# A three-line reordering in the first attention of a vision-transformer tower: where side work stands among a chunk's score matmuls

## The chip, the core and the metric

The kernel runs on one core of a Trainium2 chip. The core has five engines that run their own instruction streams in order and meet only at semaphores: TensorE (PE in the profile: matmuls and transposes, with its weight loads shown as PEld), VectorE (DVE), ScalarE (ACT), GpSimd (POOL) and SyncE (SP, which here only issues DMAs). The metric is the time on the device in microseconds, median over several executions.

## The reference, cut to what matters

The whole program is a tokenizer (two convolutions), an attention with ReLU scores, an attention per expert, a linear attention and a mixture-of-experts feed-forward, on 128 images with 64 tokens of 256 features. The change touches only the first attention:

```python
h = h + _L0_attn_ref(_layernorm(h, axis=-1), Wq, Wk, Wv, w_mlp, b_mlp)

def _L0_attn_ref(x, Wq, Wk, Wv, w_mlp, b_mlp):      # B=128, L=64, 8 groups of 32 features
    Q, K, V = x @ Wq.T, x @ Wk.T, x @ Wv.T
    Qg = Q.reshape(B, L, 1, G, Dg)
    Kg = K.reshape(B, 1, L, G, Dg)
    diff = Qg - Kg
    attn = jnp.einsum('bqkgd,d->bqkg', jax.nn.relu(diff), w_mlp) + b_mlp[0]
    attn = jax.nn.relu(attn)
    attn = jax.nn.softmax(attn, axis=2)
    Vg = V.reshape(B, L, Dg, G)
    out = jnp.einsum('bqkg,bkdg->bqdg', attn, Vg)
    return out.reshape(B, L, d_att)
```

A score is thus not a product of query and key. For every pair of tokens it is a weighted sum over 32 features of ReLU(query - key). These differences are elementwise work for VectorE, GpSimd and ScalarE, and TensorE sums them over the features.

## The kernel before, in words

`relu_attention` (lines 307 to 767) works on eight blocks of 16 images. A block has eight chunks of eight query tokens each, so there are 64 chunks, and one loop (line 708, variable `n`) runs over them. Loop `n` computes the scores of chunk `n`, and beside them the softmax of chunk `n - 1` (`old`) and the queries of chunk `n + 1`. The whole loop is written in an order fixed by hand (`tc.manual_schedule()`): every engine carries out its share of the steps in the order of the program text.

**The scores of a chunk.** 16 images times two halves of the features give 32 parts. A part is `m`, a tile of query-key differences, and it comes in one of three ways: `larger` (line 527; VectorE, max of query and key, L530, for images 0 to 7 and images 12 and 13 of the second half), `difference` (line 534; GpSimd subtracts, L538, and ScalarE applies the ReLU in place, L539) and `by_query` (line 543; ScalarE alone, four instructions of L548 per call). `begin` (line 523) starts the sum `sc` in PSUM with a full-array matmul (L525), and eight calls of `add` (line 556) sum four parts each with matmuls in 32-column strips of the array (L340, eight instructions in the trace per call). `add(i, hf)` reads the parts of images `i` to `i + 3` of feature half `hf`. `add(12, 1, True)` ends a chunk's scores.

**The softmax of the chunk before.** `less_max` (L564 to L566, VectorE) reads the finished `sc`; `exponents` (L571, ScalarE); `sums` (L574, L575, VectorE); `weights` (L578, GpSimd); `transpose` (L587, TensorE: 32 instructions in 64-column strips into a PSUM tile `pt`); `transposed` (L595, ScalarE copies it out).

**The queries of the chunk after.** `queries` (L463, TensorE, eight full-array instructions into `pc`) and `queried` (L474, ScalarE copies a part of them for GpSimd and `by_query`).

**The work of blocks.** What is done once per block is cut into steps and hung into the loops: `at(n, place, ...)` notes it, and `do(n, place)` carries it out. The places are letters. X, Y and Z hold TensorE steps. O, A, B and C hold ScalarE steps, mostly the copies out of PSUM of what X, Y and Z made, and normalisations. V1 and V2 hold VectorE steps. W holds GpSimd factors. From loop 4 to loop 59 the contents repeat every eight loops; written for loops 28 to 35:

| loop | X | Y | Z | A | others |
|---|---|---|---|---|---|
| 28 | keys (0,0) | | keys (1,0) | copies X | O copies a transpose; C normalises |
| 29 | keys (0,1) | | keys (1,1) | copies X | O copies Z of 28; C normalises |
| 30 | values 0 | key_sums | | copies X | O copies Z of 29; C normalises |
| 31 | values 1 | | values 2 | copies X | V1 correction; C normalises |
| 32 | transpose 0 | values 3 | transpose 1 | copies X | O copies Z of 31; B copies Y; V1 offsets |
| 33 | outcome 0 | outcome 1 | | copies half of X | O copies Z of 32; B and C copy more |
| 34 | back 0 | back 1 | transpose 2 | normalises | O copies the last outcome; B normalises; V2 adds |
| 35 | back 2 | back 3 | transpose 3 | normalises | O copies Z of 34; B normalises; V1 and V2 add |

Keys are four matmul instructions of 512 columns (L409), values eight of 256 (L428), a transpose four of 128 (L397), `back` four of 128 (L502), all on the full array; `outcome` is 128 small ones on 64x32 pieces (L484); key_sums are 36 in 32-column strips. From loop 43 on, the expert attention hangs its first steps into the same places (lines 1187 to 1217): the loads of its weights (loop 55, Z, L807 to L815: one memset on GpSimd and six DMAs issued by SyncE; loop 57, Z, L822: two DMAs), `wt.values` (58, Z, L833), its router's logits (61, X, L955), the first pair's queries and keys (61 Z and 62 X, L1019) and values (62 Z and 63 X, L1041). The values of loop 63 are read in that loop's V1 by VectorE (`values_kept(1)`, L1055).

**Buffers.** X, Y, Z and the transposes of the weights take their PSUM tiles from one ring of four (`sh.ps`, line 303, tag "pq"). The parts of `difference` and of the last `larger` share five buffers (`mgp`), the other `larger` have three (`mvp`), `by_query` three (`map_`), `sc` two.

**The order on each engine in one loop**, before the change:

- TensorE: `add(0,0)`, X, `add(8,0)`, `add(4,0)`, queries, Y, `add(8,1)`, `add(0,1)`, `add(4,1)`, `begin` of the next chunk, transposes of the weights, `add(12,0)`, Z, `add(12,1)`.
- ScalarE: ReLU(8,0), O, by_query(14) first half, ReLU(10,0), exponents, by_query(14) second half, ReLU(8,1), A, ReLU(10,1), queried, B, by_query(15) first half, ReLU(12,0), by_query(15) second half, ReLU(14,0), the copy of the transposed weights, C.
- VectorE: larger(0,0), larger(4,0), less_max, V1, larger(0,1), sums, larger(4,1), larger(12,1), V2.
- GpSimd: difference(8,0), (10,0), (8,1), (10,1), (12,0), weights, W, difference(14,0).

Of the kernel before, what the change touches and what calls it, by code (L numbers as in the profile page):

```python
# [306 lines left out]
def relu_attention(c, sh, wqkv, wmlp, bmlp, beside):  # L307
# [10 lines left out]
    with (  # L318
# [288 lines left out]
        def first(x):  # L607

            for half in range(2):
                for n in range(4 * half, 4 * half + 4):  # L610
                    x.statistics(n)
                x.factors(4 * half, 4 * half + 4)
            for half in range(2):
                x.offsets(4 * half, 4 * half + 4)
            for n in range(4):
                x.normal(n)
                x.normal(4 + n, True)
            for i in (0, 2, 1, 3):
                x.transpose(i)
                x.transposed(i, i > 1)  # L620
            for s in range(2):
                x.keys(s, 0)
                x.keyed(s, 0, s == 1)
            x.queries(0)
            x.queried(0)

        def first_rest(x):
            for s in range(2):
                x.keys(s, 1)
                x.keyed(s, 1, True)  # L630
            x.key_sums()
            x.correction()

        for b, x in enumerate(blocks):
            n = 8 * b
# [64 lines left out]
        def do(n, place):  # L700
            for step in work.pop((n, place), ()):
                step()

        with tc.manual_schedule():
            seq = [(x, q0) for x in blocks for q0 in range(0, T, 8)]
            first(blocks[0])
            ch, old = Chunk(*seq[0]), None
            for n in range(len(seq)):
                new = None
                ch.difference(8, 0)  # L710
                ch.larger(mvp, 0, 4, 0)
                do(n, "O")
                if n == 0:
                    first_rest(blocks[0])
                    ch.begin()
                ch.by_query(14, 1, 0)
                ch.add(0, 0)
                do(n, "X")
                ch.difference(10, 0)
                ch.add(8, 0)  # L720
                ch.larger(mvp, 4, 4, 0)
                ch.add(4, 0)
                if old:
                    old.less_max()
                    old.exponents()
                ch.by_query(14, 1, 1)
                if n + 1 < len(seq):
                    seq[n + 1][0].queries(seq[n + 1][1])
                ch.difference(8, 1)
                do(n, "A")  # L730
                do(n, "V1")
                do(n, "Y")
                ch.difference(10, 1)
                if n + 1 < len(seq):
                    seq[n + 1][0].queried(seq[n + 1][1])
                    new = Chunk(*seq[n + 1])
                do(n, "B")
                ch.by_query(15, 1, 0)
                ch.add(8, 1)
                ch.larger(mvp, 0, 4, 1)  # L740
                ch.add(0, 1)
                if old:
                    old.sums()
                ch.difference(12, 0)
                if old:
                    old.weights()
                do(n, "W")
                ch.by_query(15, 1, 1)
                ch.larger(mvp, 4, 4, 1)
                ch.add(4, 1)  # L750
                if new:
                    new.begin()
                if old:
                    old.transpose()
                ch.larger(mgp, 12, 2, 1)
                do(n, "V2")
                ch.difference(14, 0)
                if old:
                    old.transposed()
                do(n, "C")  # L760
                ch.add(12, 0)
                do(n, "Z")
                ch.add(12, 1, True)
                old, ch = ch, new
            old.less_max()
# [1403 lines left out]
@with_exitstack  # L2169
def vit_tower(ctx: ExitStack, tc: tile.TileContext, a, out):  # L2170
    const = ctx.enter_context(tc.tile_pool(name="const", bufs=1))
    dram = ctx.enter_context(tc.tile_pool(name="dram", bufs=1, space=DRAM))
    c = Ctx(tc, const)

    hd = dram.tile([B, T, D], F32, name="hd")

    hx = dram.tile([B, T, D], F32, name="hx")
    gfd = dram.tile([B * T, 1], F32, name="gfd")
    with tc.tile_pool(name="stream", bufs=1) as sp:
        c.h2 = sp.tile([P, B // 2, D], F32, name="h2")  # L2180
        tokenizer(c, a["x"], a["w1"], a["bn1"], a["w2"], a["bn2"])
        with ExitStack() as rings:
            sh = Shared(c, rings)
            beside, rest = expert_attention(
                c, sh, hd, *(a[k] for k in ("normw", "wr", "br", "wqkvf", "wvf", "wproj", "bproj", "wout"))
            )
            rest(*relu_attention(c, sh, a["wqkv0"], a["wmlp"], a["bmlp"], beside))
    c.tables(ctx.enter_context(tc.tile_pool(name="tables", bufs=1)))
    with tc.tile_pool(name="gate", bufs=1) as gp:
        k = Routing(c, gp, a["wg"], a["bg"])  # L2190
        linear_attention(c, hd, hx, out, k, a["wqk1"], a["bqk1"], a["wv1"], a["bv1"], a["wg"])
        experts(c, hx, gfd, out, a["we1"], a["we2"], a["be2"], lambda: route(c, k, gfd))
# [71 lines left out]
```

## Time and profile before

| what | us |
|---|---|
| median of 7 executions (2690.27 to 2695.7) | 2692.04 |
| the profiled execution, its own time | 2694.02 |
| its span, first to last instruction | 2692.3 |
| mean granted TensorE clock in it | 0.982 |
| VectorE's wait for scores (L564 for L340), 202 to 1110 us | 46.7 |
| TensorE busy, 560.1 to 673.7 us (eight loops, 113.6 us) | 112.45 |
| VectorE busy in the same stretch | 106.55 |
| ScalarE busy in it | 99.82 |
| GpSimd busy in it | 99.84 |

The start of `less_max` (L564) marks the loops best, since it is where VectorE meets TensorE. From the timeline, with the idle time of VectorE just before it:

| loop | start of less_max | until the next | idle before it |
|---|---|---|---|
| 28 | 601.49 | 15.16 | none |
| 29 | 616.65 | 14.59 | 1.21 |
| 30 | 631.24 | 12.97 | 1.72 |
| 31 | 644.21 | 14.86 | none |
| 32 | 659.07 | 14.59 | 1.66 |
| 33 | 673.66 | 13.30 | none |
| 34 | 686.96 | 14.00 | 0.44 |
| 35 | 700.96 | 14.11 | 0.47 |
| 36 | 715.07 | | none |

In the lines of the timeline below, the first number is the start in us from the start of the span, the second the busy time of the row, then the engine, the line of the program, the operation, output and input, their shapes and how many instructions the row merges. In brackets stands the idle time before it and what released it. A matmul row's busy time overlaps the next row a little, since matmuls are pipelined; the distance from start to start (the "step") is what TensorE spends.

### The profile page before, as it was taken

What the parts mean: (1) busy time and instruction counts of PE and PEld (TensorE: products, weight loads), DVE (VectorE), ACT (ScalarE), POOL (GpSimd) and SP (SyncE); (2) the same over time, 40 slices, a digit from 0 to 9 for tenths busy, and PEclk for the clock granted to TensorE, in tenths of its full rate; (3) what the DMA queues carried; (4) which work ended last, traced back from release to release, by engine and by line L of the source; (5) the groups of instructions that cost most, each with busy time, mean ns of one, the idle gap of its engine ahead of it and who ended that gap; (6) DMA issues with size and microseconds to landing.
All of it is one profiled execution on the core that took longest, in us unless ns stands there. A gap on an engine that the chain in (4) does not pass through costs nothing.

```text
span 2692.3 us, 80911 instructions
## 1 busy us (share of the span) xinstructions
PE 2545.4 (95%) x35229; PEld 1721.7 (64%) x35229; DVE 2025.6 (75%) x3028; ACT 1627.6 (60%) x3421; POOL 1616.5 (60%) x1381
## 2 busy tenths in 40 slices
PE   8989999999999999999999999999799986999997
PEld 4553444444443444588888888888466565888886
DVE  5759999999999989888877878777367686444443
ACT  2228888888888988766666666666245533232332
POOL 3318888888888988666666566653132312445544
PEclk9999999999999999999999999999899998999998
DMA  3100000000000000000000000000435444555554
GB/s 111 32 13 1 2 2 2 1 2 1 2 2 1 2 12 2 3 12 19 11 12 19 12 19 11 11 19 11 118 64 125 94 119 149 178 196 188 196 187 135
DMA packets 138271, 141.14 MB, mean 52 GB/s; under 512 B 107875, under 2 KB 121701, under 8 KB 130224
## 3 DMA queue, kind: packets, MB, share of 16 engines
q1 hardware_dynamic: 127536, 118.40, 14.8%
q0 software_dynamic: 7648, 14.77, 1.8%
q8 instruction: 278, 4.55, 0.7%
q10 hardware_dynamic: 2720, 2.69, 0.3%
q14 instruction: 89, 0.73, 0.1%
HBM read 104.03 MB, written 32.54 MB: 51 GB/s over the span
## 4 chain that ended last, share of the span: by engine, by line
PE 70%; DVE 19%; issue 5%; ACT 4%; POOL 2%; DMA 1%; DVEq 0%; POOLq 0%; SPq 0%; ACTq 0%
PE sc L340 12%; PE po L2108 6%; DVE m L530 6%; PE ph L2092 6%; PE pc L184 5%; PE pt L1102 4%; PE pqk L1019 4%; PE sc L1066 4%; PE pq L1426 4%; PE pv L1041 3%; PE pz L1115 3%; PE pt L587 2%; PE sc L525 2%; DVE mx L1078 2%; PE pv L1440 2%
## 5 line engine op out<-in xcount | busy, mean ns | idle before, releaser
L538 POOL TENSOR_TENSOR m<-q,k 128x1024 f32<-128x1024 f32 x384 | 718.8, 1904 | 28.8 <-PE sc L340 14.3
L530 DVE TENSOR_TENSOR m<-pc,k 128x2048 f32<-128x2048 f32 (+1 forms) x320 | 647.0, 2057 | 0.5 <-ACT q L474 0.5
L340 PE MATMUL sc<-m,wide 128*32 128x512 f32 x4096 | 528.6, 599 | 14.1 <-DVE m L530 8.9
L539 ACT ACTIVATE m<-m 128x1024 f32<-128x1024 f32 x384 | 402.7, 1050 | 10.3 <-POOL m L538 9.7
L340 PEld LDWEIGHTS sc<-m,wide 128*32 128x32 f32 x4096 | 126.2, 109 | 254.8 <-issue 140.8
L548 ACT ACTIVATE m<-k,q 128x64 f32<-128x64 f32 x1024 | 270.8, 339 | 0.9 <-DVE k L421 0.9
L1078 DVE TENSOR_REDUCE mx<-sc 128x16 f32<-128x1024 f32 x128 | 156.0, 1219 | 134.2 <-PE sc L1066 134.2
L1093 POOL TENSOR_TENSOR e<-e,mx 128x1024 f32<-128x1024 f32 x128 | 243.5, 1902 | 10.0
L1025 ACT COPY kr<-pqk 128x512 f32<-128x512 f32 x254 | 137.9, 604 | 141.1 <-PE pqk L1019 141.1
L2092 PE MATMUL ph<-xt,w1s 128*128 128x256 f32 x896 | 198.8, 380 | 3.7 <-DVE xt L2083 2.7
L2108 PE MATMUL po<-w2s,hT 128*128 128x256 f32 x896 | 198.0, 379 | 0.0
L1092 POOL TENSOR_TENSOR mx<-mx,gate 128x16 f32<-128x16 f32 x128 | 27.6, 216 | 277.7 <-ACT z L1123 162.2
L2092 PEld LDWEIGHTS ph<-xt,w1s 128*128 128x128 f32 x896 | 169.8, 190 | 28.3 <-DVE xt L2083 3.3
L2108 PEld LDWEIGHTS po<-w2s,hT 128*128 128x128 f32 x896 | 168.1, 190 | 21.7
L1105 ACT COPY pT<-pt 128x512 f32<-128x512 f32 x256 | 139.0, 600 | 51.3 <-PE pt L1102 51.1
L1079 DVE TENSOR_TENSOR e<-sc,mx 128x1024 f32<-128x1024 f32 x128 | 156.7, 1224 | 4.4
L2126 POOL DMA_INDIRECT out<-y,rout x56 | 56.7, 1013 | 167.8 <-ACT hT L2096 124.8
L1085 DVE TENSOR_REDUCE mx<-e 128x16 f32<-128x1024 f32 x128 | 152.5, 1191 | 4.6 <-ACT e L1082 4.4
L1102 PE MATMUL pt<-ident,e 128*128 128x128 f32 x1024 | 143.0, 282 | 10.3 <-DVE vr L1055 7.3
L2096 ACT ACTIVATE hT<-ph,w1s 128x256 f32<-128x256 f32 x224 | 93.0, 470 | 96.9 <-PE ph L2092 96.9
L2113 ACT ACTIVATE y<-y,gf 128x256 f32<-128x256 f32 x56 | 28.0, 507 | 196.5 <-issue 107.6
L1082 ACT ACTIVATE e<-e 128x1024 f32<-128x1024 f32 x128 | 139.6, 1091 | 1.6 <-DVE e L1079 1.6
(330 smaller groups left out, 5011.2 us busy)
## 6 DMA issues: line engine op xcount, KB each, us to landing
w1s<-in_we SPq DMA_DIRECT2D x30, 1028.0 KB, 5.2
w2s<-in_we SPq DMA_DIRECT2D x30, 1024.0 KB, 4.9
hd<-h SPq DMA_DIRECT2D x16, 512.0 KB, 3.2
x<-hd SPq DMA_DIRECT2D x16, 512.0 KB, 3.9
h<-hd SPq DMA_DIRECT2D x4, 2048.0 KB, 12.7
hx<-h SPq DMA_DIRECT2D x4, 2048.0 KB, 11.8
out<-h SPq DMA_DIRECT2D x4, 2048.0 KB, 20.6
xt<-in_x SPq DMA_DIRECT2D x15, 512.0 KB, 3.6
```

The costliest lines, as they stand in the source:

```text
L340: nc.tensor.matmul(dst[j : j + 32], wide[:, hf, s : s + 32], part, start=start, stop=stop)
L530: nc.vector.tensor_tensor(m, bcast(self.pq[:, hf, i : i + n], 3, T), k, ALU.max)
L538: nc.gpsimd.tensor_tensor(m, bcast(self.q[:, hf, s : s + 2], 3, T), k, ALU.subtract)
L539: nc.scalar.activation(m, m, AF.Relu)
L548: nc.scalar.activation(self.parts[i, hf][:, q], self.blk.k[:, hf, i], AF.Relu, bias=self.q[:, hf, i - NB // 2, q : q + 1], scale=-1.0,)
L1078: nc.vector.tensor_reduce(mx, sc, AX.X, ALU.max)
L1079: nc.vector.tensor_sub(e, sc, bcast(mx, 2, T))
L1085: nc.vector.tensor_reduce(self.sm[x], self.e[x], AX.X, ALU.add)
L1093: nc.gpsimd.tensor_mul(e, e, bcast(sm, 2, T))
L1102: nc.tensor.transpose(pt[:, cq, :], e[:, i : i + 2, :].rearrange("p e s -> p (e s)"), c.ident)
L2092: nc.tensor.matmul(ph[:, j], self.w1[:, w0 : w0 + P], self.xt[:, fc], start=(fc == 0), stop=(fc == 1))
L2108: nc.tensor.matmul(po, self.hT[:, f, r * P : r * P + P], self.w2[:, f, :], start=(f == 0), stop=(f == 7))
```

## The change

Three of the `do` lines move; nothing else does. X goes from behind `add(0,0)` to just before the queries, so `add(0,0)`, `add(8,0)` and `add(4,0)` follow one another. A goes from behind difference(8,1) to just before B, that is behind difference(10,1) and `queried`. Z goes from between `add(12,0)` and `add(12,1)` to directly behind the transposes of the weights, ahead of the last `larger`, V2, difference(14,0), the copy of the transposed weights and C.

```diff
                 ch.add(0, 0)
-                do(n, "X")
                 ch.difference(10, 0)
                 ch.add(8, 0)
                 ch.larger(mvp, 4, 4, 0)
...
                 ch.by_query(14, 1, 1)
+                do(n, "X")
                 if n + 1 < len(seq):
                     seq[n + 1][0].queries(seq[n + 1][1])
                 ch.difference(8, 1)
-                do(n, "A")
                 do(n, "V1")
                 do(n, "Y")
                 ch.difference(10, 1)
                 if n + 1 < len(seq):
                     seq[n + 1][0].queried(seq[n + 1][1])
                     new = Chunk(*seq[n + 1])
+                do(n, "A")
                 do(n, "B")
...
                 if old:
                     old.transpose()
+                do(n, "Z")
                 ch.larger(mgp, 12, 2, 1)
                 do(n, "V2")
                 ch.difference(14, 0)
...
                 do(n, "C")
                 ch.add(12, 0)
-                do(n, "Z")
                 ch.add(12, 1, True)
```

The order on TensorE becomes `add(0,0)`, `add(8,0)`, `add(4,0)`, X, queries, Y, `add(8,1)`, `add(0,1)`, `add(4,1)`, `begin`, transposes of the weights, Z, `add(12,0)`, `add(12,1)`. On ScalarE, A now stands between `queried` and B.

## The prediction

> **What bounds the kernel now.** I first read the page's table of engines, then the waits of the first attention (202 to 1110 us), then its timeline engine by engine. On the page TensorE is busy throughout, which by itself says nothing about where one stage waits.
>
> ```profile
> PE 2545.4 (95%) x35229; PEld 1721.7 (64%) x35229; DVE 2025.6 (75%) x3028; ACT 1627.6 (60%) x3421; POOL 1616.5 (60%) x1381
> ```
>
> The waits say it: of VectorE's idle time in this stage that has a releaser, all but 0.5 us is one wait, `less_max` (L564) for the scores of the chunk before.
>
> ```profile
> DVE pc L564 <- PE sc L340: 46.7, 42, 3.1
> ```
>
> 46.7 us in 42 of 64 chunks bounds what any relief of TensorE can give; in the other 22 chunks VectorE alone sets the pace. The timeline of TensorE through loop 29 (keys in X and in Z) shows a bound TensorE: start, duration, engine, line.
>
> ```profile
> 615.50 1.92 PE L340 MATMUL sc<-m,wide 128*32 128x512 f32 x16
> 617.35 1.98 PE L409 MATMUL pk<-xT,w 128*128 128x512 f32 x4
> 619.26 1.92 PE L340 MATMUL sc<-m,wide 128*32 128x512 f32 x16
> 621.12 1.16 PE L463 MATMUL pc<-xT,w 128*128 128x128 f32 x8
> 622.21 2.89 PE L340 MATMUL sc<-m,wide 128*32 128x512 f32 x24
> 642.19 2.78 PE L340 MATMUL sc<-m,wide 128*32 128x512 f32 x24
> 644.90 1.99 PE L428 MATMUL pv<-w,xT 128*128 128x256 f32 x8
> ```
>
> Starts follow one another without a hole, but each change of form costs something. Score groups: 24 matmuls step 2.71 (642.19 to 644.90), 16 step 1.85, so 8 cost 0.86 and leaving the scores costs 1.85 - 2 x 0.86 = 0.13. A foreign group of four keys steps 1.91; four of an unbroken run of keys cost 1.77 (eight in 3.53, next fence), so its way back costs 0.14 to 0.2. Projections that follow projections are nearly free: the queries step 1.09 between scores and 0.89 between keys.
>
> ```profile
> 195.54 1.05 PE L463 MATMUL pc<-xT,w 128*128 128x128 f32 x8
> 196.43 3.60 PE L409 MATMUL pk<-xT,w 128*128 128x512 f32 x8
> 199.96 0.65 PE L340 MATMUL pkb<-k,wide 128*32 128x64 f32 x32
> ```
>
> ScalarE, across loops 30 and 31, shows what X hides today: after the transposes of the weights come a copy, a normalisation, the ReLU of difference(8,0), `by_query`, and only then the ReLU of difference(10,0), over at 646.24.
>
> ```profile
> 642.31 0.59 ACT L595 COPY at<-pt 128x512 f32<-128x512 f32 x1 [1.33 <-PE pt L587]
> 642.79 0.60 ACT L388 ACTIVATE xn<-h,nb,rs 128x256 f32<-128x256 f32 x1
> 643.29 1.05 ACT L539 ACTIVATE m<-m 128x1024 f32<-128x1024 f32 x1
> 644.24 1.06 ACT L548 ACTIVATE m<-k,q 128x64 f32<-128x64 f32 x4
> 645.20 1.05 ACT L539 ACTIVATE m<-m 128x1024 f32<-128x1024 f32 x1
> ```
>
> **The sum, part by part.** It is made in differences of one profiled execution (span 2692.3, its own time 2694.02, which is 1.98 above the median of 2692.04); I set the difference against the median. In a loop, t is the start of `add(0,0)`, and `less_max` can start at t + 0.29 (616.36, which is 615.50 + 0.86, to 616.65). One cycle of eight loops (28 to 35) stands for seven.
>
> *X into the queries.* The matmuls are the same. Gone are one way out of the scores (0.13) and the way back of X (0.14 to 0.2): 0.3 per loop with keys or values. With `outcome` (64x32 tiles) only the way out is sure: 0.13 to 0.3, I take 0.2, between the two.
>
> *Z behind the transposes.* One split of the last scores goes: 0.13. How weight transposes (128x64) pass into a full projection is not in the trace: the reverse, `begin` into them, has 1.05 for two matmuls of 0.43 (0.19 over); the present way into scores ends a step of 1.09. Bounds: Z saves 0.13 + 0.19 or, with a drain of its own, nothing; I take 0.13, nearest to the split seen.
> Summed over the stage: 61 loops with X at up to 0.3 and some 45 with Z at 0.13 give 24 us of TensorE at most. The Trainium skill's "TensorEngine Tiling (Array Packing)", Key Properties, says that changing the tiling mode drains TensorE, and "TensorE: Matmul & The Clock Gate", Part 2, puts a drain at about 128 cycles, 0.05 us at 2.4 GHz; an estimate from that page is 0.1 for the two changes that an X loses and 8 us in all. The measured steps decide for 0.3.
>
> *What X covered.* `add(8,0)` reads both ReLUs. Transposes to the end of the second ReLU take 4.06 us (642.19 to 646.25). TensorE needs from there two score groups and `add(0,0)`, 2.57, and a Z, if there was one. Behind a Z of keys or values (1.9) ScalarE is in time within 0.1; behind a short Z or none, TensorE arrives 1.0 to 1.6 early, and X no longer fills that. A half-served `add` then costs a full 0.86. I walk the cycle (loop: old period to new):
> - 28, ends on VectorE's `larger(4,1)` (0.32 of waiting at 609.45): only Z counts, -0.1.
> - 29, bound by TensorE: -0.3 -0.13, +0.08 for the ReLU: -0.35.
> - 30, VectorE sets the pace: 644.21 has no wait; 0.
> - 31, no Z in 30: `add(8,0)` stands 1.55. X saves 0.3, Z 0.13, and the later A a wait of 0.35 for ReLU(10,1) behind 649.77; 0.77 is left. The 0.3 that X saves in loop 30, where VectorE paces, lets TensorE start this loop ahead and counts here: +0.5.
> - 32, VectorE paces it: 0, apart from the next part.
> - 33, short Z before: today ReLU(10,0) is over 1.74 after t and X of 1.41 covers it; `add(8,0)` will stand 1.0, less 0.2 for X and 0.3 saved in loop 32: +0.5.
> - 34: today `add(8,0)` waits until 689.51 and `add(8,1)` another 0.45 for a ReLU behind A's normalisation; A later removes the second: -0.45.
> - 35, VectorE: 0.
> Together +0.1, times seven: +0.7 us (with X at 0.13 and Z at 0, or X at 0.3 and Z at 0.32, some 0.6 a cycle up or down: -4 to +5).
>
> *A two steps on.* It leaves ReLU(10,1) and `queried` 0.47 to 0.95 earlier on ScalarE; behind them `by_query(15)`, the ReLUs of 12 and 14 and the next copy of weights come as late as before, since `queried` now waits for X and the queries. Nothing reads A's copies before the next loop but Z's transposes of rows that A and B normalise, 3 us later. The buffers: PSUM has four "pq" tiles, taken in the order X, Y, weights, Z as before; the tightest is loop 33 (four `outcome` tiles), where the weights' transposes take A's tile some 4 us after A. Price 0; without that margin, 0.47 in each of seven such loops, 3.3. The Trainium skill's "PSUM — Partial Sum Buffer", Summary: rules for kernel authors, asks to evacuate promptly and so speaks against A's delay; by it the sum would be 3.3 us higher, but no row shows a wait for such a tile.
>
> *POOL's queue.* difference(8,1) of a loop starts 1.21 after the last chunk's `add(12,0)` does (684.94, then 686.15). Z now delays that by 0.6 or 1.9; POOL has 1.4 to 3.2 us idle before its `weights`: nothing. But VectorE's `offsets` (L375) shows POOL's phase:
>
> ```profile
> 660.68 1.82 DVE L375 SCALAR_TENSOR_TENSOR nb<-mv,rs 128x4 f32<-128x4 f32 x1
> 603.68 0.52 DVE L375 SCALAR_TENSOR_TENSOR nb<-mv,rs 128x4 f32<-128x4 f32 x1
> 651.28 11.21 POOL L538 TENSOR_TENSOR m<-q,k 128x1024 f32<-128x1024 f32 x6
> ```
>
> Both end with a POOL instruction of 1.87 (651.28 + 6 x 1.87 = 662.5). In loop 32 L375 now starts 3.62 after `add(12,0)` does (two score groups 1.72, 0.29 to `less_max`, 1.61 from 659.07 to 660.68), and POOL's instruction ends at 1.21 + 2 x 1.87 = 4.95: 1.4 instead of 1.82, -0.45 on VectorE's path, in five loops: -2.3 (bounds 0.15 and 1.85 each: -8 to 0).
>
> *Loop 63.* V1 there holds `values_kept(1)`, which reads X of the same loop.
>
> ```profile
> 1096.89 1.10 PE L1041 MATMUL pv<-xTr,xnr 64*64 64x128 f32 x32
> 1098.16 1.29 DVE L1055 TENSOR_TENSOR vr<-pv,xTr 128x512 f32<-128x512 f32 x2
> ```
>
> Now X comes behind `add(8,0)` (ReLU at 1098.13, so to 1099.04) and `add(4,0)` (1099.90), plus 0.13 and 1.0: VectorE waits until about 1101.2, 3.0 later, with `larger`, the row sums and POOL's `weights` queued behind. Nothing covers it: the stage ends 3.0 later.
>
> *Loops 55 and 57* move eight small DMAs on SP and one POOL memset of 0.15 ahead of difference(14,0): their data is used in loop 58 or later and the longest lands in 3.9 us: 0.15 at most, taken as 0. Loop 0 is VectorE's: 0.
>
> Sum: +0.7 - 2.3 + 3.0 = +1.4 us, so **2693.4 us**.
>
> **Rivals.**
> *ScalarE in time (faster).* If the ReLU of 10 comes before TensorE needs it, loops 31 and 33 lose nothing: 31 gains 0.7, 33 its 0.4 of waiting, the others as above: -2.0 a cycle, -14 in seven, -2.3, +3.0: -13, 2679. For it: 46.7 us of VectorE waiting and up to 24 us of saved TensorE. Against: 4.06 against 2.57 in loop 31.
> *The ring ScalarE-TensorE (slower).* ReLU(10,0), `add`s, X, queries, `add`s, weights' transposes, copy, ReLU is now one closed chain with X inside it; with X and Y of 1.7 it comes to 13.7 to 14.6, as long as VectorE's 13.0 to 14.6. If ScalarE runs 0.5 later than put in five loops of a cycle (`queried` now blocks its queue until X and queries are done): 35 x 0.5 = 17.5, and 1.4: +19, 2711. From 0.11 each (35 x 0.11 + 1.4 = 5.3) the kernel is slower by more than 0.2%.
> *Nothing to see.* VectorE's own work (106.55 of 113.60 us of a cycle) hides both sides; this is near my sum.
>
> **How the numbers follow.** About 0.2% (5.4 us) can be told from no change. The sum and the null together: 0.42 (0.06 of it faster, 0.28 within, 0.08 slower). ScalarE in time: 0.25. The ring: 0.33, above the other since each engine here has under 1.5 us to spare in a loop and the chain grows. So faster 0.31, within 0.28, slower 0.41. The range reaches to both rivals, less a tenth at each end: 2680 to 2709; the sum's own, from its bounds (-4 to +5, -8 to 0, +3.0), is 2683 to 2700.
>
> **What would show it.** TensorE's timeline has X and queries adjoining at 0.03 apart and one run of 24 score matmuls behind Z. `add(8,0)` is split, with an idle gap before its second half, in loops 31 and 33 (gaps of 1.0 to 1.6 right; none: the faster rival). ReLU(10,1) stands before A's copy. L375 in loop 32 takes 1.4. L1055 waits 3 us for L1041. VectorE's wait for scores falls little. I am wrong if transposes-to-ReLU is not 4.06, or if ScalarE waits long at L474 in most loops.

## The result, and the profile after

The kernel after takes 2703.13 us (median; 2696.06 to 2707.3), the kernel before beside it 2692.92 (2689.53 to 2697.22): a ratio of 1.0035, 95% interval [1.0028, 1.0042]. It is slower by 10.2 us. Forecast were 2693.4 within 2680 to 2709, and "slower" as the likeliest of three outcomes; so sign and range hold, and the forecast lies 9.7 us low; taken as changes, +1.4 was forecast and +10.2 measured, 8.8 us apart. The profiled execution spans 2702.2 us and took 2703.95 itself (2692.3 and 2694.02 before).

TensorE did get cheaper. Its line on the page after:

```profile
PE 2533.0 (94%) x35229; PEld 1726.9 (64%) x35229; DVE 2023.3 (75%) x3028; ACT 1624.8 (60%) x3421; POOL 1617.6 (60%) x1381
```

From the first `less_max` to the last, TensorE is busy for 866.18 us instead of 876.98, yet that stretch takes 900.05 us instead of 890.73. VectorE is busy 2.65 us less and idle 11.97 more there. The waits of the first attention (202 to 1120 us, so that the last `less_max`, at 1118.01, is inside) say where: engine, line, what it waited for, us in all, times, longest.

```profile
DVE pc L564 <- PE sc L340: 56.5, 39, 3.1
...
ACT q L474 <- PE pc L463: 23.8, 37, 2.5
...
PE po L484 <- issue: 5.8, 7, 1.1
...
DVE vr L1055 <- PE pv L1041: 2.4, 1, 2.4
```

The wait for scores grew by 9.8 us, from 46.7, and L1055 has a new wait of 2.4; together that is about what VectorE is idle more. ScalarE now waits 23.8 us for the queries (1.8 before). And TensorE has idle time inside `outcome` (L484) which nothing released; before, no loop shows any. These are the changes of each loop's period, from one `less_max` to the next. Predicted and measured, in us; measured are the regular cycles:

| loop | 28 | 29 | 30 | 31 | 32 (with L375) | 33 | 34 | 35 | 63 |
|---|---|---|---|---|---|---|---|---|---|
| predicted | -0.1 | -0.35 | 0 | +0.5 | -0.45 | +0.5 | -0.45 | 0 | +3.0 |
| measured | -0.13 | -0.50 | -0.12 | +0.55 | -0.47 | +1.28 to +2.04 | -0.23 | 0 | +2.49 |

One loop in eight stands out: the place of loop 33, where both outcomes are written. Its seven occurrences (9, 17, ... 57) add up to 12.6 us where 3.5 were priced. That difference of 9.1 us is as large as the miss of 8.8; what the other loops were off by nearly cancels (-3.3 measured from first to last `less_max`, -2.1 priced).

TensorE after, through loop 31 and into 32:

```profile
644.50 3.63 PE L340 MATMUL sc<-m,wide 128*32 128x512 f32 x28
648.61 1.91 PE L340 MATMUL sc<-m,wide 128*32 128x512 f32 x12 [0.47 <-ACT m L539]
650.45 1.99 PE L428 MATMUL pv<-w,xT 128*128 128x256 f32 x8
652.28 1.05 PE L463 MATMUL pc<-xT,w 128*128 128x128 f32 x8
...
658.11 1.99 PE L428 MATMUL pv<-w,xT 128*128 128x256 f32 x8
660.03 4.57 PE L340 MATMUL sc<-m,wide 128*32 128x512 f32 x40
```

X (650.45) and queries adjoin; behind the transposes and Z (658.11), the last 16 score matmuls of the loop run on into the next loop's 24. In loop 31 `add(8,0)` is the stretched end of the group of 28 and the wait of 0.47 for the ReLU. And loop 33:

```profile
673.99 5.41 PE L340 MATMUL sc<-m,wide 128*32 128x512 f32 x40
679.33 1.48 PE L484 MATMUL po<-at,v 64*32 64x64 f32 x128
680.74 1.16 PE L463 MATMUL pc<-xT,w 128*128 128x128 f32 x8
681.83 0.44 PE L484 MATMUL po<-at,v 64*32 64x64 f32 x28
682.76 1.20 PE L484 MATMUL po<-at,v 64*32 64x64 f32 x100 [0.49 <-issue]
```

Two things cost here. Forty score matmuls take 5.41 us instead of the 4.57 of loop 32: 0.84 in which `add(8,0)` is half served, without an idle gap of its own. And Y, only eight matmuls behind X, stops after 28 of its 128 matmuls. The same loop in the kernel before had X inside the scores, and 24 matmuls (16 of scores, eight of the queries) between X and Y:

```profile
674.32 1.49 PE L484 MATMUL po<-at,v 64*32 64x64 f32 x128
675.73 1.92 PE L340 MATMUL sc<-m,wide 128*32 128x512 f32 x16
677.59 1.16 PE L463 MATMUL pc<-xT,w 128*128 128x128 f32 x8
678.67 1.49 PE L484 MATMUL po<-at,v 64*32 64x64 f32 x128
```

ScalarE after, in loop 31: ReLU(8,1) and ReLU(10,1) (L539 x2) stand ahead of the queries' copy and A's copy, as the change says, and the queue stands for 1.45 us until the queries are there.

```profile
649.93 1.99 ACT L539 ACTIVATE m<-m 128x1024 f32<-128x1024 f32 x2
653.37 0.27 ACT L474 COPY q<-pc 128x128 f32<-128x128 f32 x1 [1.45 <-PE pc L463]
653.53 0.59 ACT L439 COPY v<-pv 128x512 f32<-128x512 f32 x1
```

VectorE after: the offsets in loop 32, and loop 63.

```profile
663.67 1.36 DVE L375 SCALAR_TENSOR_TENSOR nb<-mv,rs 128x4 f32<-128x4 f32 x1
...
1107.34 1.29 DVE L1055 TENSOR_TENSOR vr<-pv,xTr 128x512 f32<-128x512 f32 x2 [2.41 <-PE pv L1041]
```

### The profile page after: what moved, and what is told of

Its sections match the earlier page's. It is cut to its first block, busy times and chain, and to the rows that moved or that the text cites. A ratio compares the mean times of both kernels' runs of the same rounds, so it can differ in the third digit from the quotient of the medians.

```text
span 2702.2 us, 80909 instructions
## 1 busy us (share of the span) xinstructions
PE 2533.0 (94%) x35229; PEld 1726.9 (64%) x35229; DVE 2023.3 (75%) x3028; ACT 1624.8 (60%) x3421; POOL 1617.6 (60%) x1381
## 3 DMA queue, kind: packets, MB, share of 16 engines
q8 instruction: 278, 4.55, 0.7%
## 4 chain that ended last, share of the span: by engine, by line
PE 69%; DVE 18%; issue 5%; ACT 5%; POOL 2%; DMA 1%; POOLq 0%; DVEq 0%; SPq 0%; ACTq 0%
PE sc L340 11%; PE po L2108 6%; PE ph L2092 6%; DVE m L530 6%; PE pc L184 5%; PE pt L1102 4%; PE pqk L1019 4%; PE sc L1066 4%; PE pq L1426 4%; PE pv L1041 3%; PE pz L1115 3%; PE pt L587 2%; PE sc L525 2%; PE pv L1440 2%; PE pk L409 2%
## 5 line engine op out<-in xcount | busy, mean ns | idle before, releaser
L340 PE MATMUL sc<-m,wide 128*32 128x512 f32 x4096 | 518.4, 597 | 28.8 <-DVE m L530 17.0
L539 ACT ACTIVATE m<-m 128x1024 f32<-128x1024 f32 x384 | 396.3, 1048 | 10.2 <-POOL m L538 10.2
```

Of the source, the lines that this page charges most:

```text
L340: nc.tensor.matmul(dst[j : j + 32], wide[:, hf, s : s + 32], part, start=start, stop=stop)
L539: nc.scalar.activation(m, m, AF.Relu)
```

## The experiments

Theory after the result: (1) A and Z gain, X loses; (2) in loop 33 X's loss has two parts, the lost cover of `add(8,0)` and a shortage of instructions, since two outcomes of 128 matmuls and 128 weight loads each now come close together ("supply"). Rivals: the coupling of X to ScalarE costs everywhere; or the cover alone explains loop 33.

Times are given against the kernel before run beside each (2692.64 for the first four, 2690.36 for the next four, 2691.82 for the last two).

### One part at a time

X alone:

```diff
                 ch.add(0, 0)
-                do(n, "X")
...
                 ch.by_query(14, 1, 1)
+                do(n, "X")
```

> Only X moves; A and Z stay where they were. Theory (X does the harm: it no longer covers the ReLU before add(8,0), and in the loops with outcome TensorE's two groups of small matmuls stand close together): the loss of the whole change is X's, and A, which stays ahead of the ReLU of difference(10,1), now makes ScalarE wait for the late X. At least the 10 us of the whole change: +12 to +25 us, the loops with outcome 14.5 or longer instead of 13.3. Rival (A's delay does the harm, its copies hold up what follows): X alone costs 3 us at most, which is loop 63.

Measured 2738.49, ratio 1.0167 [1.0150, 1.0184]: +45.9, nearly twice the upper end expected. The loops of 29, 30 and 31 are longer by 1.28, 0.84 and 1.62, loop 33 by 1.4 to 2.9, loop 63 by 4.5. VectorE's wait for scores is 90.4 us. ScalarE shows why, one line of ScalarE and one of TensorE:

```profile
636.79 0.59 ACT L421 COPY k<-pk 128x512 f32<-128x512 f32 x1 [1.16 <-PE pk L409]
```

```profile
634.76 1.98 PE L409 MATMUL pk<-xT,w 128*128 128x512 f32 x4
```

A's copy, still ahead of ReLU(10,1), waits 1.16 us for the late X, and `add(8,1)` waits for that ReLU: the 24 score matmuls behind the queries take 3.58 us, against 2.89 before. A late X without a late A thus costs far more than the whole change.

Z alone:

```diff
                     old.transpose()
+                do(n, "Z")
...
                 ch.add(12, 0)
-                do(n, "Z")
```

> Only Z moves. Theory: loops 28, 29 and 31 of each cycle lose one break of the scores, 0.13 each, and offsets in loop 32 fall from 1.82 to about 1.4 by GpSimd's phase: -2.5 to -6 us in all. Rival (Z delays the last scores and with them GpSimd's difference(8,1) on a path that counts): 0 to +5 us.

Measured 2682.75, ratio 0.9962 [0.9948, 0.9976]: -9.9, more than the 2.5 to 6 expected. The loops of 28, 29, 31, 33 and 34 are each shorter by 0.14, which is the 0.13 priced for one way out of the scores; loop 32 by 0.47, which is L375 at 1.36 instead of 1.82. Together 1.17 a cycle, 8.2 in seven; the expectation had left out loops 33 and 34.

A alone:

```diff
                 ch.difference(8, 1)
-                do(n, "A")
...
                     new = Chunk(*seq[n + 1])
+                do(n, "A")
```

> Only A moves. Theory: with X early, the later A lets the ReLU of difference(10,1) pass ahead of a copy: loops 31 and 34 gain 0.35 and 0.45 each, -2 to -6 us in all. Rival (A's delay does the harm): +5 to +12 us, loops with outcome 14 or longer.

Measured 2683.49, ratio 0.9966 [0.9954, 0.9979]: -9.2, more than the 2 to 6 expected. Loops 31 and 34 gain 0.36 and 0.39, as priced (0.35 and 0.45). Loop 32 gains 0.86, which was not priced: L375 takes 0.33 there.

### Loop 33

X back to its old place in loops 9, 17, ... 57 of the kernel after:

```diff
+                early = n % 8 == 1 and n > 8
+                if early:
+                    do(n, "X")
                 ch.difference(10, 0)
...
                 ch.by_query(14, 1, 1)
-                do(n, "X")
+                if not early:
+                    do(n, "X")
```

> The changed kernel, but in the seven loops with outcome (9, 17, ... 57) X goes back between add(0,0) and add(8,0). Theory: those loops return from about 15.1 to 13.3, 1.3 to 1.9 each: 9 to 13 us under the changed kernel, so within 3 us of the kernel before, and no idle time of TensorE inside outcome is left. Rival (the loss is spread over all loops as one ring): 2 us under the changed kernel at most.

Measured 2690.22, ratio 0.9988 [0.9978, 0.9998]: -2.4, 12.6 below the kernel after. The seven loops are back at 0.14 under before and TensorE has no idle time inside `outcome`. So against before, the loss of 10.2 us sits in these seven loops; what the late X costs in the others is made up there by what A and Z gain (below). That does not yet part cover from supply.

Y apart from X in the same loops:

```diff
                 do(n, "V1")
-                do(n, "Y")
+                apart = n % 8 == 1 and n > 8
+                if not apart:
+                    do(n, "Y")
...
                 ch.add(0, 1)
+                if apart:
+                    do(n, "Y")
```

> The kernel after, but in the seven loops 9, 17, ... 57 (the place of loop 33) the second outcome, Y, is issued behind add(0,1) instead of 6 instructions behind the first, X. Theory 'supply' (two outcomes of 128 small matmuls and 128 weight loads each, back to back, outrun what feeds TensorE's instructions): the idle time inside the outcome that has no releaser, 0.5 to 1.1 us in each of these loops, goes; the cover of add(8,0) stays lost (0.8 each). So these loops are 0.5 to 1.1 shorter than in the kernel after and 0.6 to 1.0 longer than before; in all 4 to 7 us under the kernel after, 2696 to 2699. Rival 'cover alone' (the loops are longer only because TensorE's work is missing in front of the second half of the scores): they stay 1.3 to 2.0 longer than before, and the time within 2 us of the kernel after. If Y at its new place itself lies on the path, the loops get longer by up to its 2.3 us.

TensorE in loop 25, the place of loop 33:

```profile
556.43 5.41 PE L340 MATMUL sc<-m,wide 128*32 128x512 f32 x40
561.78 1.49 PE L484 MATMUL po<-at,v 64*32 64x64 f32 x128
563.19 1.16 PE L463 MATMUL pc<-xT,w 128*128 128x128 f32 x8
564.28 1.92 PE L340 MATMUL sc<-m,wide 128*32 128x512 f32 x16
566.14 1.48 PE L484 MATMUL po<-at,v 64*32 64x64 f32 x128
```

With 24 matmuls between X and Y again, Y runs through without a hole, while the scores ahead of X still take 5.41. Five of the seven loops are 0.78 longer than before, one 0.87 and one 1.82 (loop 49: there the group of eight score matmuls right behind Y took 2.20 instead of 1.06 at a full granted clock). So the loops without Y's nearness are 0.78 longer than before, and what Y's nearness added was 0.5 to 1.3. In the time this is not to be told from the kernel after: 2698.74, ratio 1.0030 [1.0021, 1.0040], so +8.4 against +10.2. That is within the 2 us that the rival "cover alone" allowed: the loops of the one profiled execution speak against the rival, the median does not, and the next kernel has to decide. In the profiled execution the stretch from first to last `less_max` is 4.4 us shorter than in the kernel after, although loop 44 is 1.6 longer (below).

The converse, on the kernel before: X stays early, Y is put right behind it.

```diff
                 ch.add(0, 0)
                 do(n, "X")
+                joined = n % 8 == 1 and n > 8
+                if joined:
+                    do(n, "Y")
...
-                do(n, "Y")
+                if not joined:
+                    do(n, "Y")
```

> The kernel before, but in the loops 9, 17, ... 57 the second outcome, Y, is issued directly behind the first, X, at X's old place. X, A and Z stand as before. Theory 'supply': idle time of 1 to 2.2 us with no releaser appears inside the second outcome in each of these loops, though nothing else is late there (the kernel before shows 2.18 us in its one pair of outcomes back to back, behind the loops). Time: these loops 0.5 to 2 longer than before, 2696 to 2707. Rival 'cover alone': no such idle time; the cover of add(8,0) is 2.3 us longer than before, and the loops change by -0.3 to +0.3, so 2690 to 2695.

Measured 2707.05, ratio 1.0060 [1.0043, 1.0077]: +16.7, at the upper edge of what "supply" gave. The seven loops are longer by 1.82 to 2.00 (two of them 3.75 and 3.86), 17.2 in all; every other loop is within 0.02 of before. In the two, loops 57 and 41, the 16 score matmuls behind the stop take 3.37 and 3.48 us instead of 1.92: the granted clock is 0.50 from 800 to 802 us in loop 41, and from 1032 to 1034 in loop 57. TensorE in loop 25:

```profile
562.48 2.67 PE L484 MATMUL po<-at,v 64*32 64x64 f32 x248
567.05 0.32 PE L484 MATMUL po<-at,v 64*32 64x64 f32 x8 [1.91 <-issue]
```

Here nothing was moved but Y, and nothing that it reads is late: 248 matmuls run, then TensorE stands for 1.91 us with no releaser. "Cover alone" falls. What fits is instruction supply. The transfers of the same kernel between 562 and 568 us, busy tenths of the DMA engines in 40 slices of 0.15 us:

```profile
DMA  0000000000000000030000000000000000000000
...
q8 instruction: 1, 0.02, 0.9%
```

One packet, of the queue that carries instructions, in the slice from 564.55 on; TensorE resumes 2.5 us after it. The same holds for all 40 stops with no releaser inside or right behind a second `outcome` in the traces of this case (eight each here, in the kernel after, in X alone and in X and A below; one in each other kernel, behind the loops): a packet of q8 starts 2.2 to 2.9 us ahead of the resumption, while in this stage such packets come only every 12 us or so (74 between first and last `less_max`). Where the stop falls changes from loop to loop (in the kernel after, Y has issued 19 to 106 of its 128 matmuls) and is the same in the same loop of the kernel after, of X alone and of X and A; that speaks against a wait for a PSUM tile, which would stand at one place of `outcome`. The page of the kernel after gives the size:

```profile
span 2702.2 us, 80909 instructions
...
q8 instruction: 278, 4.55, 0.7%
q14 instruction: 89, 0.73, 0.1%
```

A packet of q8 has 4.55 MB / 278 = 16.4 KB; all 5.28 MB over 80,909 instructions are 65 bytes each, so by estimate a packet holds some 250 instructions: one `outcome`, of 256, which TensorE gets through in 1.42 us. The profile does not say for which engine a packet is, but the count fits TensorE: between first and last `less_max` of the kernel after it has 9,430 matmuls and 9,432 weight loads, 255 for each of the 74 packets of q8. That packets which take over 2.2 us to become work set the stop remains an inference, since nothing here varies the packets themselves. That a second `outcome` close behind the first stops TensorE, and that 24 matmuls between them take the stop away in most loops, is shown. Not in all: in loop 49 of the kernel with Y apart, the weight loads of the score matmuls behind Y stand for 1.00 us with no releaser (0.30 in the fastest kernel's loop 49) and resume at 911.72, 2.35 us after a packet of q8, so by its marks the long group there is the same stop.

The kernel before had this stop too, behind the loops, where two outcomes stand back to back; the row was there to be read:

```profile
1115.24 1.96 PE L484 MATMUL po<-at,v 64*32 64x64 f32 x175 [0.69 <-ACT at L595]
1119.38 1.04 PE L484 MATMUL po<-at,v 64*32 64x64 f32 x81 [2.18 <-issue]
```

### Which parts to keep

A and Z moved, X at its old place everywhere:

```diff
                 ch.add(0, 0)
+                do(n, "X")
...
                 ch.by_query(14, 1, 1)
-                do(n, "X")
```

> A and Z are moved as in the change, X stands at its old place in all loops. With Z alone the time fell by 9.9 us and with A alone by 9.2. Theory 'places add up': per cycle -0.14 (28), -0.25 (29), 0 (30), -0.5 (31), -0.5 to -1.3 (32), -0.1 (33), -0.5 (34), 0 (35) = -2.0 to -2.8: 2673 to 2679. Rival 'the gains overlap': 2680 to 2685. And against the kernel that keeps X late in three loops of eight: if X late is worth anything by itself in the loops 28, 29 and 30, this one is slower by 1 to 3 us; if not, level.

Measured 2677.40, ratio 0.9949 [0.9932, 0.9965]: -13.0. By loops -0.14, -0.25, 0, -0.50, -0.47, -0.14, -0.55, 0: 2.05 a cycle, at the lower edge of what "places add up" gave. By the medians the gains of A and Z (9.2 and 9.9 alone) overlap by 6; by the time from first to last `less_max` in the profiled executions (9.80 and 8.17 shorter alone, 14.54 together) by 3.4.

X late only in the three loops of eight in which the kernel after was level or shorter:

```diff
+                early = n % 8 not in (4, 5, 6) or n < 4 or n > 55
+                if early:
+                    do(n, "X")
                 ch.difference(10, 0)
...
                 ch.by_query(14, 1, 1)
-                do(n, "X")
+                if not early:
+                    do(n, "X")
```

> The kernel after, but X is issued behind add(0,0) as before in all loops except those of remainder 4, 5 and 6 by 8, where the kernel after was level or shorter (by 0.12 to 0.50). A and Z are moved as in the change. Theory 'places add up' (each loop's change stands for itself): per cycle about -0.1 -0.5 -0.1 -0.4 -0.5 0 -0.4 0 = -2.0 to -2.8, so 14 to 20 us under before: 2673 to 2679. Rival 'the gains of the single parts overlap' (the moved A and the moved Z each gained some 9 us alone, but on the same waits): 2680 to 2685.

Measured 2673.41, ratio 0.9933 [0.9917, 0.9950]: -17.0, and the fastest of all here. Loops 29 and 30 (-0.50, -0.13) are where a late X gains 0.25 and 0.13 against the last kernel, which is 4.0 us slower (1 to 3 were expected if a late X is worth anything there).

X and A, without Z:

```diff
-                do(n, "Z")
                 ch.larger(mgp, 12, 2, 1)
...
                 ch.add(12, 0)
+                do(n, "Z")
```

> X and A are moved as in the change, Z stands at its old place. X alone cost 46 us, A alone gained 9, A and Z together gained 13. Theory 'A rescues X' (X late costs most because the copies of A, ahead of ReLU(10,1) on ScalarE, wait for it): with A behind ReLU(10,1) most of the 46 is gone, and Z is worth 3 to 4 more beside A, so 13 to 17 us over before: 2704 to 2708. Rival 'Z does it' (X and Z compete for TensorE, and it is Z's move that makes room): the time stays near that of X alone less A's 9, so 2725 to 2735.

Measured 2721.77, ratio 1.0107 [1.0086, 1.0128]: +30.0, between both expectations. So A's move is worth 16 us beside X (45.9 to 30.0), and Z's another 20 (30.0 to 10.2), though each gains 9 to 10 alone. Both repair what X breaks: with Z at its old place, loops 29, 30 and 31 are 0.48, 0.58 and 0.81 longer than before, with Z moved -0.50, -0.12 and +0.55. Why Z is worth that much beside X is not settled by a run; ScalarE's wait for the queries, 38.2 us here, 23.8 with Z moved, goes the same way.

### GpSimd's phase

L375 took 1.82 us before, 1.36 in the kernel after, 0.33 with A alone. GpSimd's rows and VectorE's L375 with A alone:

```profile
645.41 11.22 POOL L538 TENSOR_TENSOR m<-q,k 128x1024 f32<-128x1024 f32 x6
```

```profile
654.45 0.33 DVE L375 SCALAR_TENSOR_TENSOR nb<-mv,rs 128x4 f32<-128x4 f32 x1
```

Six differences of 1.87 us run through, the fifth to 645.41 + 5 x 1.87 = 654.76; L375 ends at 654.78. In the fastest kernel a wait for scores parts them:

```profile
642.29 5.63 POOL L538 TENSOR_TENSOR m<-q,k 128x1024 f32<-128x1024 f32 x3
648.69 5.63 POOL L538 TENSOR_TENSOR m<-q,k 128x1024 f32<-128x1024 f32 x3 [0.77 <-PE sc L340]
```

There L375 starts at 651.11 and the second difference behind the wait ends at 648.69 + 2 x 1.88 = 652.45; L375 takes 1.36, to 652.47. So in both it ends with a difference of GpSimd, as in the kernel before: by these rows its length follows GpSimd's phase.

The next kernel puts Z of the loops of 31 back, on top of the fastest:

```diff
-                do(n, "Z")
+                if n % 8 != 7:
+                    do(n, "Z")
...
                 ch.add(12, 0)
+                if n % 8 == 7:
+                    do(n, "Z")
```

> The kernel with X early but in three of eight loops (16.9 us under before), and Z at its old place in the loops of remainder 7 by 8 (the place of loop 31) as well. There the offsets of L375 took 0.33 us with A alone and 1.36 with A and Z, because GpSimd, which waited 0.77 us for scores in loop 31, is still in its products when VectorE comes to L375. Theory 'Z in loop 31 sets GpSimd's phase': L375 falls to 0.33 in loop 32 (so -1.0 there, less 0.1 to 0.3 that the loops 31 and 32 give back), five to six times: 2668 to 2672. Rival 'the phase comes from elsewhere' (Z in the loops before, or X): L375 stays at 1.36, loop 31 loses the 0.14 of Z: 2673.5 to 2675.

The mechanism is as the first theory has it: GpSimd's six differences run through again, the fifth to 650.68, L375 takes 0.41, and loop 32 is 1.00 under before (0.47 without this).

```profile
641.33 11.21 POOL L538 TENSOR_TENSOR m<-q,k 128x1024 f32<-128x1024 f32 x6
```

```profile
650.29 0.41 DVE L375 SCALAR_TENSOR_TENSOR nb<-mv,rs 128x4 f32<-128x4 f32 x1
```

The time is not: 2679.33, ratio 0.9948 [0.9927, 0.9968], above both expectations. Loops 31 and 33 give back 0.15 and 0.18, so a cycle gains only 0.2, and in the profiled execution loop 44 is 1.6 longer than in the fastest kernel (the clock, below) and loop 49 0.6: there the 24 score matmuls behind Y take 3.50 us instead of 2.91, with 0.59 us of idle time on the weight loads (0.30 otherwise) that nothing released and that ends 2.4 us after a packet of q8. Why the median lost is open.

## Why the prediction was right, and where it was not

- **Sign and range** were right; the slower outcome had the largest chance. In good part that is luck. The single time, 2693.4, rested on a sum of +1.4 where +10.2 was measured, and the sum's own range, 2683 to 2700, leaves the result out. The stated range holds it because it reached to the ring rival, and "slower" had 0.33 of its 0.41 from that rival, whose path is not what the runs show.
- **Loop 33 is the term that was mis-sized**: "`add(8,0)` will stand 1.0, less 0.2 for X and 0.3 saved in loop 32: +0.5". With Y apart the loop measured +0.78: of the 0.5 of savings set against the 1.0, some 0.2 shows. A and Z alone make the loop 0.14 shorter; what became of the rest of the 0.5 no run shows. The rest, 0.5 to 1.3 a loop, has no term at all: moving X to the queries put it eight matmuls ahead of Y, and two outcomes that close stop TensorE. The sum counted how long X's matmuls take and how many forms they change, not how many instructions come per microsecond. The ring rival asked for 0.5 us in each of 35 loops, and for 0.11 to be told from before; the loss lies between, but sat in seven loops.
- **Loop 31** (+0.5, measured +0.55), **29** (-0.35, -0.50), **28** (-0.1, -0.13), **35** (0, 0): right. X's own saving, priced at 0.3, is the 0.25 that a late X gains in loop 29. Transposes to the end of ReLU(10,0) is 4.05 us after, 644.50 to 648.55, as the 4.06 read before. The gaps named as the sign were 1.0 to 1.6; what shows is one of 0.47 in loop 31 and none in loop 33, where the group is stretched (5.41 for 4.57): the half-served `add` hides in the groups' durations, and a missing gap was no sign that ScalarE is in time.
- **Z at 0.13**: right to 0.01 in five loops of eight, by Z alone. I had noted that by "TensorEngine Tiling (Array Packing)" of the Trainium skill, Key Properties, a change of tiling mode drains TensorE. The runs agree that changing costs something, and price one split of the scores at 0.14 us.
- **L375 at 1.4**: measured 1.36, in the kernel after, with Z alone, and in the fastest. The row's rule (it ends with a difference of GpSimd) held. What I did not see is that it can go to 0.33.
- **A**: its waits in loops 31 and 34 were priced rightly (0.35 and 0.45; alone 0.36 and 0.39), though in the kernel after loop 34 keeps only 0.23, since there TensorE now stands 0.94 us in `add(8,0)` for a ReLU (0.22 before). The rest of the move was put at nothing; alone it also brings 0.86 in loop 32, by L375. The Trainium skill's "PSUM — Partial Sum Buffer", Summary: rules for kernel authors, spoke against evacuating later; in this case the later evacuation gained, and no run shows a wait for such a tile.
- **Loop 63 at +3.0**: L1055 waits 2.41, the loop is 2.49 longer. With X early there (the fastest kernel) it is level with before.
- **X's whole price** beside A and Z is 23.2 us (+10.2 against -13.0). By loops, kernel after less the kernel of A and Z: 29 -0.25, 30 -0.13, 31 +1.05, 33 +1.9 on average, 34 +0.3, so 2.9 a cycle, some 20 in seven, and 2.5 in loop 63.
- **VectorE's wait for scores** was to fall a little; it rose from 46.7 to 56.5.
- **L474**: the prediction called itself wrong "if ScalarE waits long at L474 in most loops". It waits in 37 of 64, 0.64 on average, so the sign came true. That wait alone is no price: the kernel of A and Z waits there 23 times, 12.1 us in all, and is 13 us faster than before.

## What to carry to other kernels

When a group of many small instructions is moved, ask what other such group it comes to lie beside: here 256 instructions run in 1.42 us, and a second 256 close behind stop TensorE for 0.5 to 2.2 us with no releaser, and 24 other matmuls between them took the stop away in most loops. A row "idle, released by nothing" anywhere in a trace, even outside the stage in question, is a price list for that. And a change of several moves is best tried move by move: two of these three gained, and the third cost more than both.

## What the runs showed that I had not expected

- The stop of TensorE inside `outcome`, above: 1.5 to 2.2 us for two outcomes back to back, 0.5 to 1.2 with eight matmuls between them, none inside `outcome` with 24, though in loop 49 a shorter one can follow right behind it (1.0 and 0.6).
- A fall of TensorE's granted clock can follow a wait of 1.92 us, and need not. The same wait, in loop 44 of the kernel with Z of the loops of 31 put back, and then of the fastest:

```profile
823.83 1.72 PE L340 MATMUL sc<-m,wide 128*32 128x512 f32 x8 [1.92 <-DVE m L530]
825.49 2.07 PE L525 MATMUL sc<-kb,ident 128*128 128x512 f32 x2
```

```profile
825.22 1.06 PE L340 MATMUL sc<-m,wide 128*32 128x512 f32 x8 [1.92 <-DVE m L530]
826.21 1.13 PE L525 MATMUL sc<-kb,ident 128*128 128x512 f32 x2
```

The windows from 822 to 826 and from 826 to 830 us of the first, then of the second; the granted clock is the number after GpSimd's busy time:

```profile
822.00:826.00 4.00, 2.17 (x9) 0.66 (x10) 3.93 (x7) 2.28 (x6) 4.00 (x3) 0.76 0.00 0
826.00:830.00 4.00, 4.00 (x38) 1.69 (x36) 4.00 (x2) 1.31 (x3) 2.42 (x2) 0.81 0.00 0
```

```profile
822.00:826.00 4.00, 2.06 (x18) 0.32 (x16) 3.96 (x5) 2.60 (x8) 2.82 (x2) 1.00 0.01 2
826.00:830.00 4.00, 4.00 (x42) 1.99 (x38) 3.93 (x7) 2.59 (x4) 3.81 (x3) 1.00 0.00 0
```

In the first the clock falls to 0.76 and the next two groups take 3.79 us instead of 2.19: 1.6 us. The kernel with Y apart has the same in loop 44 (clock 0.66 from 838 to 842), and so has the one with X early at the place of loop 33 (0.72 from 836 to 840). The Trainium skill's "TensorE: Matmul & The Clock Gate", Part 1, puts the fall after an idle window of about 3.4 us; here eight kernels have the wait of 1.92 us in loop 44: in three of them the clock fell behind it, in five it stayed at 1.00. What decides between them is not shown.
